# Seven-product scores for one more pair of query tiles in a causal attention and expert kernel

## The chip, the core and the metric

One core of a Trainium2 chip runs the whole program. Its engines are TensorE (PE, with weight loads as PEld), VectorE (DVE), ScalarE (ACT), GpSimd (POOL) and SyncE (SP), which here only issues DMAs. The metric is the time of one execution on the device in microseconds; less is better.

## The reference

All in float32. `x` has 2 batches of 2048 rows of 512. The normalised rows go through causal attention (with a norm of its own ahead of it) and through a mixture of 8 experts (width 352, the 2 best of each row); the result is `x + s * silu(experts)`.

```python
xn = _layernorm(x, axis=-1)
# attention
x_norm = (xn - mu) / jnp.sqrt(var + EPS) * gamma + beta
q, k, v = (x_norm @ qkv[:, i * KEY : (i + 1) * KEY] for i in range(3))
scores = jnp.einsum('bsk,btk->bst', q, k) * scale
scores = jnp.where(causal[None], scores, -jnp.inf)
attn = jax.nn.softmax(scores, axis=-1)
s = (attn @ v) @ o_proj + xn
# experts
h = jax.nn.silu(jnp.einsum('td,ehd->teh', xf, w1) + b1)
y = jnp.einsum('teh,edh->ted', h, w2) + b2
g = _silu(jnp.einsum('ted,te->td', y, comb))
x = x + s * g
```

## The kernel before

The program goes through norms and projections, then routing and experts (rows gathered by expert, 68 slots), and then the attention, the last 420 us or so. The change is in the attention alone.

**Tiles and steps.** A query tile is 128 rows. `seq` orders the 32 tiles, and the attention loop has a step `s` for each: the first batch's tiles 15 down to 0 in steps 0 to 15, then the second batch's in pairs, before in the order (8, 9), (0, 1), (6, 7), (2, 3), (4, 5), (10, 11), (12, 13), (14, 15), steps 16 to 31. Tile t needs keys 0 to t: whole blocks of 512 columns, and one cut block. `K` is 4, the first key block of the second batch, so K to K+3 are its four blocks.

**One step.** In step s TensorE makes the scores of tile s (`chunk_scores`, L994: four matmuls for a block), VectorE masks the last 128 columns (L999) and takes the maximum (L982), ScalarE takes the exponentials (`exponentials`, L1138). Their transpose is made in 16-bit halves: GpSimd splits them (`pu`, L1148), SP issues a transposing DMA (`puT`), and VectorE joins them in the next step (`join_p`, L1170). Tiles of at most 384 columns (`by_te`) are turned by TensorE instead (`turn_p`, L1165), with a copy back by ScalarE (L1166). The product with the values follows two steps after the scores (`values`, L1188).

**The end of a tile.** `gate` (L1343, L1344 on VectorE, then silu on ScalarE, L1346) combines the two gathered expert rows of a pair three steps after the pair's first tile, at the end of the step. `attended` (L1351 on ScalarE, then L1354 on VectorE) scales the attention's result three steps after its tile, and a step later `emit` (L1362, L1363 on GpSimd) multiplies and adds, and SP stores. `gather_y` (L1333) gathers expert rows from GpSimd's queue. exp and silu need different tables on ScalarE, so there is a table load at each change between them.

**Seven products.** For the pairs in `FAST` (0 to 3 and 13 to 15) scores against blocks 0 and 1 of a batch are made for two tiles at once as a 2 x 2 block product with seven products instead of eight (`fast_scores`, L1046, with additions on VectorE, L1052, and a copy of the first product by ScalarE, L1065). It needs four sums of the two tiles' queries (`query_sums`, L1013 to L1016) and four of the two key blocks (`block_sums`, L1027). The values of these pairs are multiplied in the same way (`values_first`, `values_next`, `values_end`, L1236), and need four sums for each value block (`combine_v`, L1210) and of the exponentials (`combine_p`, L1230).

**Buffers.** Products and scores lie in PSUM: pool `ps_a` has five banks of 128x512 float32, `ps_b` three. Each request takes the next bank of its pool and waits until the former content has been read. Before, products of steps after the third all use `ps_a`, so the sixth waits for the bank of the first. Keys have four buffers: block K's load takes the place of block 1 of the first batch, which tile 4 uses last, in step 11.

**Order.** It is written out by hand: each engine executes its instructions in the order in which the Python code gives them, and waits at the head of its queue. A step's code runs in this order: start of the step with loads of queries; `attended` and `emit` of earlier tiles; loads of `xo`; scores, with joins of the tile before between the blocks; `values` and `turn_p` where the tile before is short; the maximum's end (L1082); divisors; exponentials, with their DMAs; parts of key and value loads (`fetch_parts`, L794, at most four); the sums of keys and values that are due; the query sums for the next step; values; `gate`; `gather_y`. Before, value sums of K are made in step 20, of K+1 in step 22, of K+2 in step 26, and the key sums in steps 21 to 24, one in each:

```python
combine = {20: K, 22: K + 1, 26: K + 2}
...
            if s in combine:
                combine_v(combine[s])
            if 21 <= s < 25:

                block_sums(K, (s - 20,))
            if s % 2 and s > 3 and s // 2 + 1 in FAST:
                query_sums(s + 1, nc.vector)
```

In the second batch only pairs 13 to 15 use the sums.

Of the kernel before, what the change touches and what calls it, by code (L numbers as in the profile page):

```python
# [26 lines left out]
def gated_attention_moe(  # L27
# [27 lines left out]
    nc = tc.nc  # L55
# [752 lines left out]

    assert B == 2 and NBB == 4
    seq = [t for t in reversed(range(NBB * BT))]  # L810
    seq += [NBB * BT + t for t in (8, 9, 0, 1, 6, 7, 2, 3, 4, 5, 10, 11, 12, 13, 14, 15)]
    assert all(seq[s] // 2 == seq[s + 1] // 2 for s in range(0, NT, 2))
    fetch_k = fetch(aks, lambda: kp2, kt_d, "k2", "kT")
    fetch_v = fetch(avs, lambda: vp, v_d, "v2", "v")
# [142 lines left out]


    FAST = (0, 1, 2, 3, 13, 14, 15)

    def place(s):
        b, t = divmod(seq[s], BT)
# [21 lines left out]

    def direct(s):

        return range(2 if s // 2 in FAST else 0, len(widths[s]))

    def chunk_scores(s, j):
        b, t, first = place(s)  # L990
# [27 lines left out]
    def block_sums(first, parts=(1, 2, 3, 4)):  # L1018

        if 1 in parts:  # L1020
            bsums[first] = kt.tile([P, 4, ND // 2, TB], F32, name=f"tk_{first}", tag="tk")
        k = bsums[first]
        (b11, b12), (b21, b22) = ([aks[first + j][:, d, :] for j in range(2)] for d in kds)
        for i, x1, x2 in (1, b12, b11), (2, b22, k[:, 0]), (3, b22, b12), (4, b21, k[:, 1]):
            if i in parts:
                engine = nc.gpsimd if i == 3 and first == 0 else nc.vector
                engine.tensor_tensor(k[:, i - 1], x1, x2, ALU.subtract)  # L1027
# [103 lines left out]
    def exponentials(s):  # L1131

        _, nm, pieces = scored.pop(s)
        rs = sm.tile([P, NBB], F32, name=f"rs_{s}", tag="rs")
        sums[s], halves[s] = rs[:, : len(pieces)], []
        for j, (src, at) in enumerate(pieces):
            end = at + src.shape[1]
            nc.scalar.activation(  # L1138
                turned[s][:, at:end], src, AF.Exp, bias=nm, accum_out=rs[:, j : j + 1]
            )  # L1140
            if by_te(s):
                continue
            for k in range(at, end, TB):
                w = min(end - k, TB)

                pool, tag, n = (op, "xo", 4) if s == 1 else (php, "pu", 3)
                pu = pool.tile([P, 2 * TB], U16, name=f"pu_{s}_{k}", tag=tag, bufs=n)
                nc.gpsimd.tensor_copy(  # L1148
                    pu[:, : 2 * w].rearrange("p (h d) -> p h d", h=2),
                    turned[s][:, k : k + w].bitcast(U16).rearrange("p (d h) -> p h d", h=2),  # L1150
                )
                pool, tag, n = (op, "o", 4) if s == 1 else (php, "puT", 5)
                puT = pool.tile([P, 2 * BT, P], U16, name=f"puT_{s}_{k}", tag=tag, bufs=n)
                nc.sync.dma_start_transpose(out=puT[:, : 2 * w // P, :], in_=pu[:, : 2 * w])
                halves[s].append((puT, k, w))
# [170 lines left out]
    def gather_y(s):  # L1326

        rows[s] = [op.tile([P, 2, D], F32, name=f"yg0_{s}", tag="yg0")]
        for i in range(2):
            rows[s].append(op.tile([P, D], F32, name=f"yg1_{s + i}", tag="yg1"))  # L1330
            n = seq[s + i]
            for k, y in enumerate((rows[s][0][:, i, :], rows[s][-1])):
                nc.gpsimd.indirect_dma_start(  # L1333
                    out=y, out_offset=None, in_=y_d,
                    in_offset=bass.IndirectOffsetOnAxis(ap=posi[k][:, n : n + 1], axis=0),
                )
# [61 lines left out]
    parts_b = [(s, f, b, c) for s, f, b in parts_b for c in range(ND)]  # L1398
    parts_b.sort(key=lambda part: part[0])

    combine = {20: K, 22: K + 1, 26: K + 2}

    def fetch_parts(s, most):
        while parts_b and most and parts_b[0][0] <= s:
# [3 lines left out]

    for s in range(NT + OUT + 2):
        fast = s // 2 - 1 in FAST  # L1410
        pair = (s, s + 1) if s // 2 in FAST else (s,)
        if s < NT and (s % 2 == 0 or len(pair) == 1):
            for k in pair:
                if s:
                    begin_scores(k)
                room(k)
        n = s // 2 + 1
        if s % 2 == 0 and NQ <= n < NT // 2:
            for c in range(2):
                fetch_q(n, c)  # L1420
        if s == 0:
            fetch_parts(s, NBB * ND)
            block_sums(0)
        late = []
        for k in range(NT):
            if k not in AHEAD:
                wait = 4 - k % 2 if k // 2 in FAST else 3
                if s == k + wait:
                    late.append((attended, k))
                if s == k + wait + 1:  # L1430
                    emit(k)
        if len(pair) == 1 or s % 2:
            for f, *args in late:
                f(*args)
        for k in range(NT):
            if s == (NT - 1 if k in AHEAD else k + 2 - k % 2 if k // 2 in FAST else k + 1):
                fetch_inputs(k)
        if s == NT - 1:
            gather_y(NT - 2)
        joins = []  # L1440
        for k in () if s == 1 else (0, 1) if s == 2 else (s - 1,):
            if 0 <= k < NT - 1 and not by_te(k):
                joins += [(join_p, k)] * len(halves[k])
        chunks = []
        if s < NT and s != 1:
            chunks = [(k, j) for k in ((1,) if s == 0 else (s,)) for j in direct(k)]
        if s == 0:

            for k, j in chunks:
                chunk_scores(k, j)  # L1450
            chunks = []
        if s < NT and s % 2 == 0 and len(pair) == 2:
            pools = [(ps_b, "b")] * (NBB - 1) + [(ps_a, "a")] if s < 3 else [(ps_a, "a")]
            if s == 2:
                joins = [(combine_v, b, (1,)) for b in range(NBB - 1)] + joins
            now = 5 if s == 2 else 1
            fast_scores(s, pools, late + joins[:now])
            joins = joins[now:]
            if s == 0:
                query_sums(2, nc.gpsimd)  # L1460
        for k, j in chunks:
            chunk_scores(k, j)
            if s != 3 and joins:
                f, *args = joins.pop(0)
                f(*args)
        if s != 3:
            for f, *args in joins:
                f(*args)
        if 0 <= s - 1 < NT and by_te(s - 1):

            values(s - 2)
            turn_p(s - 1)
        if s < NT and s != 1:
            end_scores(s)
        if fast and s % 2 == 0 and 2 < s < NT:
            combine_p(s - 2)
        if 0 <= s - 1 < NT:
            divisor(s - 1)
        if s < NT:
            if s != 1:  # L1480
                exponentials(s)
            if s % 2 == 0 and len(pair) == 2:
                maximum(s + 1, turned[s + 1][:, : 2 * TB], 0)
            if s == 0:
                end_scores(1)
                exponentials(1)
            fetch_parts(s, 4)
            if s in combine:
                combine_v(combine[s])
            if 21 <= s < 25:  # L1490

                block_sums(K, (s - 20,))
            if s % 2 and s > 3 and s // 2 + 1 in FAST:
                query_sums(s + 1, nc.vector)
        if s == 2:
            pass
        elif s == 3:
            combine_p(0, (1, 3, 2))
            for b in range(NBB - 1):
                combine_v(b, (2,))  # L1500
            values_first(0)
            combine_p(0, (4,))
            for b in range(NBB - 1):
                combine_v(b, (4,))
            values_next(0)
            for f, *args in joins:
                f(*args)
            values_end(0, [lambda: query_sums(s + 1, nc.vector)])
        elif fast and s % 2 == 0:
            values_first(s - 2)  # L1510

            if s != NT - 2:
                values_next(s - 2)
        elif fast and s == NT - 1:
            values_next(s - 3)
            gate(s - 1)
            values_end(
                s - 3, [lambda: join_p(s)] * len(halves[s]) + [lambda: combine_p(s - 1)]
            )
            for k in AHEAD:  # L1520
                make_ahead(k)
        elif fast:
            values_end(s - 3)
        elif 0 <= s - 2 < NT and not (s - 1 < NT and by_te(s - 1)):
            values(s - 2)

        for k in range(0, NT - 2, 2):
            if s == (k + 2 if k + 2 in AHEAD else k + 3):
                gate(k)
        for k in range(0, NT - 2, 2):  # L1530
            if s == k + 1:
                gather_y(k)
        if s == 1:
            for b in range(NBB - 1):
                combine_v(b, (3,), nc.gpsimd)
# [45 lines left out]
```

## Time and profile before

| what | value |
|---|---|
| median of 3 runs | 1059.44 us (1057.37 to 1060.53) |
| the profiled execution | 1057.82 us |
| its span, first to last instruction | 1056.1 us |
| granted TensorE clock | 1.00 |
| TensorE idle, 860 to 890, 890 to 920, 920 to 950 us | 1.23, 1.30, 1.71 us |
| VectorE busy, 772 to 830 us | 33.1 of 58 us |
| VectorE busy, 830 to 950 us | 88.4 of 120 us |

Steps 12 to 15 run from about 795 to 820 us on TensorE, step 16 from 820, step 26 from 910, step 28 from 941.

Times of instructions are counted from the span's start. Where a line of the timeline names something in brackets, the engine stood idle for so long just before, and the name is what ended that. A float32 matmul is counted as two entries.

### The profile page before, as it was taken

What the parts mean: (1) busy time and instruction counts of PE and PEld (TensorE: products, weight loads), DVE (VectorE), ACT (ScalarE), POOL (GpSimd) and SP (SyncE); (2) the same over time, 40 slices, a digit from 0 to 9 for tenths busy, and PEclk for the clock granted to TensorE, in tenths of its full rate; (3) what the DMA queues carried; (4) which work ended last, traced back from release to release, by engine and by line L of the source; (5) the groups of instructions that cost most, each with busy time, mean ns of one, the idle gap of its engine ahead of it and who ended that gap; (6) DMA issues with size and microseconds to landing.
All of it is one profiled execution on the core that took longest, in us unless ns stands there. A gap on an engine that the chain in (4) does not pass through costs nothing.

```text
span 1056.1 us, 12196 instructions
## 1 busy us (share of the span) xinstructions
PE 1038.8 (98%) x3554; PEld 616.2 (58%) x3554; DVE 644.1 (61%) x1227; ACT 312.6 (30%) x643; POOL 432.4 (41%) x469
## 2 busy tenths in 40 slices
PE   8999999999999999999999999999999999899998
PEld 3687886444555555555545446676665544447577
DVE  4797884775333333334335459767655668688686
ACT  3222221211322322322355322122334443422330
POOL 2364250003433333334332127354547776754372
PEclk9999999999999999999999999999999999999999
DMA  8699989946999999999897257445668768744361
GB/s 302 180 283 282 282 263 339 340 142 171 221 221 227 222 233 228 223 232 218 207 187 159 58 191 180 118 101 139 184 169 270 214 202 231 185 112 120 96 156 40
DMA packets 300512, 209.33 MB, mean 198 GB/s; under 512 B 234520, under 2 KB 247576, under 8 KB 299424
## 3 DMA queue, kind: packets, MB, share of 16 engines
q1 hardware_dynamic: 281248, 146.12, 55.5%
q0 software_dynamic: 10560, 35.17, 13.0%
q10 hardware_dynamic: 8640, 27.27, 7.1%
q8 instruction: 30, 0.49, 0.2%
q14 instruction: 34, 0.28, 0.1%
HBM read 92.89 MB, written 60.03 MB: 145 GB/s over the span
## 4 chain that ended last, share of the span: by engine, by line
PE 77%; POOL 6%; issue 6%; DVE 5%; DMA 3%; ACT 2%; SPq 0%; ACTq 0%; POOLq 0%; DVEq 0%
PE py L921 16%; PE ph L882 15%; PE p L1236 9%; PE ps L994 8%; PE p L400 7%; PE p L1046 6%; PE pj L341 3%; PE pw L207 3%; PE po L1188 3%; PE pj L346 3%; PE p L1188 2%; POOL yg L1333 2%; POOL pu L1148 1%; DMA zuT<-zu 1%; POOL o L1362 1%
## 5 line engine op out<-in xcount | busy, mean ns | idle before, releaser
L921 PE MATMUL py<-w,ht 128*128 (+3 forms) x408 | 187.1, 594 | 0.0
L882 PE MATMUL ph<-w,xT 128*128 (+1 forms) x544 | 173.2, 460 | 0.7 <-POOL keep L1103 0.7
L929 DVE COPY y<-py 128x512 f32<-128x512 f32 x68 | 46.9, 690 | 179.0 <-PE py L921 172.9
L994 PE MATMUL ps<-k,q 128*128 128x512 f32 (+3 forms) x416 | 143.0, 495 | 0.0
L882 PEld LDWEIGHTS ph<-w,xT 128*128 128x128 f32 (+1 forms) x544 | 97.5, 181 | 73.1 <-issue 34.5
L907 ACT ACTIVATE ht<-ht,b1sel 128x128 f32<-128x128 f32 (+3 forms) x237 | 73.1, 375 | 224.1 <-DVE ht L901 224.1
L892 POOL COPY hu<-h 128x704 uint16<-128x704 uint16 x68 | 52.4, 771 | 204.1 <-ACT h L890 124.7
L1148 POOL COPY pu<-pT 128x1024 uint16<-128x1024 uint16 (+2 forms) x74 | 84.0, 1167 | 126.3 <-ACT pT L1138 67.3
L921 PEld LDWEIGHTS py<-w,ht 128*128 128x128 f32 (+3 forms) x408 | 73.4, 182 | 75.4 <-issue 37.4
L994 PEld LDWEIGHTS ps<-k,q 128*128 128x128 f32 x416 | 74.6, 190 | 67.6 <-issue 57.7
L768 POOL DMA_INDIRECT xs<-zu_d,toki x68 | 68.9, 1014 | 69.3 <-DVE toki L642 57.9
L1188 PE MATMUL po<-v,pT 128*128 128x512 f32 x182 | 81.2, 593 | 1.2 <-DVE pT L1170 1.2
L1333 POOL DMA_INDIRECT yg<-y_d,posi x64 | 64.2, 1003 | 36.5 <-DVE yg L1344 22.1
L264 POOL COPY zu<-z 128x1024 uint16<-128x1024 uint16 x32 | 35.2, 1100 | 78.0 <-DVE z L249 78.0
L1170 DVE COPY pT<-puT 128x1024 uint16<-128x1024 uint16 (+2 forms) x74 | 55.9, 787 | 7.4 <-DMA puT<-pu 7.4
L1188 PEld LDWEIGHTS po<-v,pT 128*128 128x128 f32 x182 | 34.0, 190 | 40.0 <-issue 37.8
L413 DVE TENSOR_TENSOR so<-p,so 128x512 f32<-128x512 f32 x70 | 45.8, 686 | 16.5 <-DMA v_d<-so 9.3
L1354 DVE SCALAR_TENSOR_TENSOR o<-xo,xscale,o 128x512 f32<-128x512 f32 x30 | 28.7, 962 | 41.9 <-ACT o L1351 17.3
L842 DVE COPY xT<-xhT 128x1024 uint16<-128x1024 uint16 x68 | 47.2, 693 | 10.6 <-PE ph L882 5.7
L1052 DVE TENSOR_TENSOR pT<-p,pT 128x512 f32<-128x512 f32 x49 | 32.8, 687 | 25.5 <-PE p L1046 13.8
L1362 POOL TENSOR_TENSOR o<-o,yg 128x512 f32<-128x512 f32 x30 | 41.8, 1393 | 13.5 <-DVE o L1354 12.5
L1138 ACT ACTIVATE pT<-ps,nm 128x512 f32<-128x512 f32 (+3 forms) x52 | 30.0, 581 | 56.6 <-DVE nm L1082 37.3
(246 smaller groups left out, 1670.5 us busy)
## 6 DMA issues: line engine op xcount, KB each, us to landing
y_d<-y SPq DMA_DIRECT2D x68, 256.0 KB
zu_d<-zu SPq DMA_DIRECT2D x32, 264.0 KB
x<-in_x_dram SPq DMA_DIRECT2D x32, 256.0 KB
kt_d<-kT ACTq DMA_DIRECT2D x8, 1024.0 KB
k<-kt_d SPq DMA_DIRECT2D x32, 256.0 KB
q<-qt_d SPq DMA_DIRECT2D x32, 256.0 KB
v<-v_d SPq DMA_DIRECT2D x32, 256.0 KB
xo<-in_x_dram SPq DMA_DIRECT2D x32, 256.0 KB
```

Of the source, the lines that this page charges most:

```text
L400: nc.tensor.matmul(ps[:, r, :], lhsT=lhs[:, c, ts(r, P)], rhs=rhs[:, c, :], start=(c == 0), stop=(c == 1),)
L768: nc.gpsimd.indirect_dma_start(out=xs, out_offset=None, in_=zu_d, in_offset=bass.IndirectOffsetOnAxis(ap=toki[:, i : i + 1], axis=0),)
L882: nc.tensor.matmul(ph[at, :], lhsT=xT[:, c, at], rhs=rhs[k], start=(c == 0), stop=(c == ND - 1),)
L907: nc.scalar.activation(ht[:hn, c, at], ht[:hn, c, at], AF.Silu, bias=b1sel[:hn, c, j : j + 1])
L921: nc.tensor.matmul(py[at, :], lhsT=ht[:k, c, at], rhs=rhs[n], start=(c == 0), stop=(c == NH - 1),)
L994: nc.tensor.matmul(ps[:, :w], lhsT=aqs[seq[s] // 2][:, c, ts(t % 2, P)], rhs=aks[first + j][:, c, :w], start=(c == 0), stop=(c == ND - 1),)
L1046: nc.tensor.matmul(ps, lhsT=x[:, c], rhs=y[:, c], start=(c == 0), stop=(c == ND // 2 - 1))
L1148: nc.gpsimd.tensor_copy(pu[:, : 2 * w].rearrange("p (h d) -> p h d", h=2), turned[s][:, k : k + w].bitcast(U16).rearrange("p (d h) -> p h ...
L1170: nc.vector.tensor_copy(turned[s][:, k : k + w].bitcast(U16).rearrange("p (i t h) -> p i t h", t=P, h=2), puT[:, : 2 * w // P, :].rearrang ...
L1188: nc.tensor.matmul(dst, lhsT=turned[s][:, ts(k, P)], rhs=avs[first + k // BT][:, k % BT, cols], start=(start and k == k0), stop=(k == k1 - 1),
L1236: nc.tensor.matmul(dst, lhsT=a[:, k], rhs=v(k), start=(k == 0), stop=(stop and k == n - 1))
L1333: nc.gpsimd.indirect_dma_start(out=y, out_offset=None, in_=y_d, in_offset=bass.IndirectOffsetOnAxis(ap=posi[k][:, n : n + 1], axis=0),)
```

## The change

Five things change.

1. Pair 8 (tiles 8 and 9 of the second batch, steps 16 and 17) gets its scores against blocks 0 and 1 by seven products (`SCORED`), in step 16; its values stay as they were. Step 17's joins of tile 16 move behind its exponentials (`behind`).
2. The short tiles 0 and 1 change places with tiles 6 and 7: they come in steps 20, 21 instead of 18, 19.
3. The sums of keys and values of the second batch are spread (`later`): values of K+2 in steps 10, 11 and 12 (one, one, two), keys in 13, 14 and 15 (one, two, one), values of K+1 in 17 to 20 and of K in 20 to 23, one in each step.
4. The query sums for a pair go ahead of the joins and scores of the step before it, instead of to its end.
5. In the seven products of steps after the third, the sixth takes a bank of `ps_b`.

```diff
@@ -808,7 +808,7 @@
-    seq += [NBB * BT + t for t in (8, 9, 0, 1, 6, 7, 2, 3, 4, 5, 10, 11, 12, 13, 14, 15)]
+    seq += [NBB * BT + t for t in (8, 9, 6, 7, 0, 1, 2, 3, 4, 5, 10, 11, 12, 13, 14, 15)]
@@ -957,6 +957,7 @@
     FAST = (0, 1, 2, 3, 13, 14, 15)
+    SCORED = FAST + (8,)
@@ -984,7 +985,7 @@
-        return range(2 if s // 2 in FAST else 0, len(widths[s]))
+        return range(2 if s // 2 in SCORED else 0, len(widths[s]))
@@ -1398,7 +1399,13 @@
-    combine = {20: K, 22: K + 1, 26: K + 2}
+    later = {}
+    for steps, f, b in (
+        ((10, 11, 12, 12), combine_v, K + 2), ((13, 14, 14, 15), block_sums, K),
+        ((17, 18, 19, 20), combine_v, K + 1), ((20, 21, 22, 23), combine_v, K),
+    ):
+        for i, step in enumerate(steps):
+            later.setdefault(step, []).append((f, b, (i + 1,)))
@@ -1408,7 +1415,7 @@
-        pair = (s, s + 1) if s // 2 in FAST else (s,)
+        pair = (s, s + 1) if s // 2 in SCORED else (s,)
@@ -1437,10 +1444,16 @@
+        if s % 2 and s > 3 and s // 2 + 1 in SCORED:
+            query_sums(s + 1, nc.vector)
         joins = []
...
+        behind = []
+        if s % 2 and s // 2 in SCORED and s // 2 not in FAST:
+
+            behind, joins = joins, []
@@ -1450,7 +1463,9 @@
-            pools = [(ps_b, "b")] * (NBB - 1) + [(ps_a, "a")] if s < 3 else [(ps_a, "a")]
+            pools = [(ps_a, "a")] * 5 + [(ps_b, "b"), (ps_a, "a")]
+            if s < 3:
+                pools = [(ps_b, "b")] * 3 + [(ps_a, "a")]
@@ -1479,19 +1494,16 @@
             if s != 1:
                 exponentials(s)
+            for f, *args in behind:
+                f(*args)
...
             fetch_parts(s, 4)
-            if s in combine:
-                combine_v(combine[s])
-            if 21 <= s < 25:
-
-                block_sums(K, (s - 20,))
-            if s % 2 and s > 3 and s // 2 + 1 in FAST:
-                query_sums(s + 1, nc.vector)
+            for f, *args in later.pop(s, []):
+                f(*args)
```

## The prediction

> **What bounds the kernel now.** I read the busy shares first, then TensorE's waits, then its timeline from 810 us on, and then the other engines' timelines at the same times.
>
> ```profile
> PE 1038.8 (98%) x3554; PEld 616.2 (58%) x3554; DVE 644.1 (61%) x1227; ACT 312.6 (30%) x643; POOL 432.4 (41%) x469
> ...
> PE p L1046 <- ACT yg L1346: 1.7, 1, 1.7
> ...
> PE p L1046 <- DVE sq L1014: 1.3, 1, 1.3
> PE po L1188 <- DVE pT L1170: 1.2, 1, 1.2
> ...
> PE p L1046 <- ACT pT L1065: 0.4, 1, 0.4
> ```
>
> The span is TensorE's. A change pays only by removing matmuls or one of these few stalls, and costs as soon as it makes a new one. Columns of a wait: total, times, longest.
>
> The price of seven products comes from the chain of waits (one fp32 matmul counts as two entries):
>
> ```profile
> 674.45 12.02 PE p L1046 x28
> ```
>
> So 14 matmuls of 128x512 take 12.02 us, 0.859 us each.
>
> What decides is how tight steps 13 to 16 are. Timeline (start, duration, what; in brackets the idle before), SyncE, VectorE, ScalarE, GpSimd, TensorE:
>
> ```profile
> 806.42 1.23 SPq L1154 DMA_TRANSPOSE puT<-pu  x1
> 807.71 2.01 SPq L794 DMA_DIRECT2D k<-kt_d  x4
> ...
> 810.52 0.47 DVE L1343 TENSOR_SCALAR yg<-yg,share 128x512 f32<-128x512 f32 x1
> ...
> 812.21 0.75 DVE L1344 SCALAR_TENSOR_TENSOR yg<-yg,share,yg 128x512 f32<-128x512 f32 x1
> 816.11 1.26 DVE L1354 SCALAR_TENSOR_TENSOR o<-xo,xscale,o 128x512 f32<-128x512 f32 x1 [3.15 <-ACT yg L1346]
> ...
> 813.06 1.28 ACT L1346 ACT_TABLE_LOAD   x1 [1.95 <-DVE yg L1344]
> 814.35 1.06 ACT L1346 ACTIVATE yg<-yg 128x1024 f32<-128x1024 f32 x1
> 815.32 0.76 ACT L1351 ACTIVATE o<-po,xshift,ri 128x512 f32<-128x512 f32 x1
> 816.67 0.48 ACT L1166 COPY pT<-pt 128x384 f32<-128x384 f32 x1 [0.60 <-PE pt L1165]
> ...
> 815.52 1.28 POOL L1362 TENSOR_TENSOR o<-o,yg 128x512 f32<-128x512 f32 x1
> ...
> 817.31 2.74 PE L1188 MATMUL po<-v,pT 128*128 128x512 f32 x6
> 820.11 7.92 PE L994 MATMUL ps<-k,q 128*128 128x512 f32 x24
> ```
>
> Read down: gate(10) on VectorE ends at 812.96, silu(10) with its table load follows, then attended(11), then the copy of tile 13's transpose, which ends at 817.15. TensorE uses it at 817.31. There are 0.6 us between attended(11) and that copy; any greater delay of gate(10) is a stall of TensorE.
>
> **What the Trainium skill says.** "SBUF — State Buffer", Who interferes with whom: a VectorE instruction with two SBUF inputs and a GpSimd instruction that reads SBUF exclude each other for the whole instruction. The trace agrees: the attended operation at 816.11 takes 1.26 us beside the GpSimd operation that ends at 816.80, and 0.75 us elsewhere; the query sum at 914.96 takes 1.26 instead of 0.42. "ScalarE: Activation LUTs", What ACT_TABLE_LOAD costs: 1.28 us, as here, at each change between silu and exp. "DMA: Bandwidth & Descriptors", Anatomy of one DMA: about 2 us are fixed; here a 256 KB xo load issued at 803.36 releases VectorE at 806.00. "PSUM — Partial Sum Buffer", The four PSUM rules: a product of 512 fp32 columns fills a bank, so five banks of ps_a hold five products, which the 1.7 us wait above shows: product six waits for the copy of product one.
>
> **The gains.** (Line numbers are those of before.)
> - Pair 8 (steps 16, 17) needs 14 matmuls instead of 16 for blocks 0 and 1: 2 x 0.859 = -1.7 us.
> - The stall of 1.2 us at 887.5 is values(20) waiting for a join that stands behind a late attended operation (2.19 us at 883.52). With the short tiles in steps 20, 21, tile 20 is turned by TensorE and has no join: -1.2. Tiles 6, 7 take steps 18, 19, and their four transposes on SP now stand ahead of keys 7's four loads. They have about 24 us from score to use: nothing.
> - In step 26, 1.3 (query sums behind a join that waits 2.13 us for its DMA) and 1.7 us (copy of product one behind silu(22)). Three key sums of 1.2 us and eight value sums of 0.7 us leave steps 20 to 23, one value sum a step returns, and the query sums (4 x 0.42) go ahead of the joins; VectorE is 3 to 5 us earlier: -3.0. The same for 0.4 us in step 28. The query sums of step 5 move into 4.3 us of idle VectorE: nothing.
> - The sixth product's other bank: no gain by itself, since the seventh needs product one's bank 1.7 us later. In steps 28 to 31 it turns the ring of three banks by one; what is then waited for was read some 10 us before: nothing.
> - The value sums of keys K+2 leave step 26 for steps 10 to 12. See the next part for those of steps 11 and 12.
>
> Sum: -6.3 us.
>
> **The costs.** They follow one chain, which I worked through by order of instructions and rows of the profile.
> 1. *Step 11.* A value sum of 0.68 us stands ahead of gate(8), where VectorE and GpSimd alternate (a GpSimd operation ends at 793.04, two copies follow). It waits for the first, gate(8) ends at about 797.8 instead of 796.0. Silu(8), attended(9) and step 12's joins follow; exp(12), its GpSimd copy, its transpose on SP and the four key loads behind that on SP come 0.7 to 2.2 us later. I take 2.2.
> 2. *Step 13.* The first key sum (L1027, 1.21 us) stands ahead of gate(10) and reads the first two quarters of keys 4. In before these are issued from 807.71; 512 KB have moved by 811.4 and, with the 0.65 us that a transpose needed from its last byte to its join, they are usable at 812.0; with 2.2 us, at 814.2. Sum until 815.4, gate(10) (2.45) until 817.8 instead of 812.96, 4.8 later. Less the slack of 0.8 (0.6 ahead of the copy, 0.2 behind it), TensorE stands 4.0 us at L1188 in step 15. Floor: no delay in step 11, 812.0 + 1.21 + 2.45 = 815.7, which is 2.7 later, a stall of 1.9.
> 3. *Steps 14, 15.* Ahead of the query sums that product three needs stand attended(11), the mask and maximum, key sums two and three (2 x 1.21), attended(12), two query sums (0.84). From attended(11) on ScalarE (A) that is A + 5.9; TensorE wants it at A + 6.9 (copy 0.5, two handoffs, values 2.6, turn 0.3, products one and two 3.4). Without disturbance: no stall. But silu(10) releases four GpSimd operations of 1.27 us, of which VectorE meets three to four: 3 us later, a stall of 2.1 us at L1046. Product four also needs the bank that exp(15) frees, about as late.
> 4. *Step 16.* Key sum four (1.21) and gate(12) (2.45) stand ahead of silu(12), and that ahead of the copy of product one: it ends 17.4 us after A, and product seven is due at 15.9 (the 2.1 included): 1.6 us more with the handoff. Floor of 3 and 4 together 0.5, ceiling 4.5.
> 5. *Step 18.* Tile 16's exponentials now wait for the products' sums: copy + 3.4 (five adds) + 0.75 + 0.7 + 1.2 (maximum of 1024) + 0.7 + 0.75 = 7.5, exp 1.15, then 4.5 to the first join, as in before (832.17 to 836.72), + 0.7. TensorE wants it 13.0 us after the copy (product seven 1.7, then 11.3 of other matmuls): 13.8 - 13.0 = 0.8 us, between 0 and 1.6. The new step 17 puts these joins behind the exponentials, so they delay no maximum.
>
> VectorE's nine more instructions (1.2 us and less) are in this chain. Sum: 4.0 + 2.1 + 1.6 + 0.8 = +8.5, between 2.4 and 11.
>
> **The sum.** -6.3 + 8.5 = +2.2 us on the profiled execution: 1057.8 (span 1056.1 and 1.7 around it) becomes 1060.0. That execution lies 1.6 us below the median 1059.4; against the median, 1061.6.
>
> **The rivals.**
> - *The gain arrives.* If step 11's sum delays nothing and GpSimd's four operations meet VectorE's gaps (it stands idle 3.15 us at 812.96 and 1.25 at 818.5), costs are 2.4 to 3.1: -6.3 + 2.7 = -3.6, 1055.8. For it: every added operation fits in VectorE's idle time by size. Against: that idle time is waiting on ScalarE, and the additions stand ahead of what ScalarE waits for.
> - *The shared SBUF read port decides* (slower). Place: VectorE between attended(11) and the query sums of step 15. If GpSimd wins each turn, key sums two and three, attended(12) and the first query sum each wait 1.27 us, and tile 16's joins meet the copies for tile 17 likewise: costs 3 to 5 rise by 3, +5.2, 1064.6. It decides from the first GpSimd operation beyond the 1.0 us of slack. For it: 883.52, where an attended operation took 2.19 us. Against: usually VectorE gets every second turn.
> - *The change doesn't do what it says at step 26*: its stalls return because VectorE is late throughout: 3.0 more than the forecast, 1064.6. Against: 9 us of sums left these steps, 3 came back. It is inside the slower case.
>
> **How the numbers follow.** 0.3% (3.2 us) is about what a measurement can tell from no change. Forecast (between -3.2 and +3.2): 0.48. Gain arrives: 0.20. Slower by the port, a longer load of keys or joins: 0.32. The range 1056 to 1065 spans -3.4 to +5.6; the forecast's own is 1056.2 to 1062.6.
>
> **What would show it.** TensorE's waits after: the three of steps 22 and 26 gone; new ones at L1188 (on ScalarE's copy) near 817 us of 2 to 4 us, at L1046 on the query sums or exp(15), and on the copy of product one. VectorE's first key sum starts on a DMA of keys 4 after 812. Wrong if tile 13's copy still ends near 817.2, if product three doesn't wait, or if the stalls of step 26 remain.

## The result and the profile after

The changed kernel takes 1064.22 us (median of 6, 1063.2 to 1066.11) against 1059.59 us of the kernel before (6 runs): a ratio of 1.0052, 95% interval 1.0039 to 1.0064. It is slower by 4.6 us. Its profiled execution took 1064.46 us, span 1062.8.

The page's first part and TensorE's waits, after (a line of code has moved by one in this region, so L1188 of before is L1189):

```profile
PE 1039.7 (98%) x3550; PEld 615.9 (58%) x3550; DVE 663.2 (62%) x1236; ACT 312.1 (29%) x640; POOL 433.9 (41%) x469
...
PE po L1189 <- ACT pT L1167: 2.9, 1, 2.9
PE p L1237 <- DVE u L1254: 2.1, 1, 2.1
...
PE po L1189 <- ACT pT L1139: 1.3, 1, 1.3
PE po L1189 <- DVE pT L1171: 1.2, 1, 1.2
PE p L1047 <- ACT pT L1066: 1.1, 2, 0.8
PE p L1047 <- ACT pT L1139: 1.0, 1, 1.0
```

TensorE has two matmuls fewer (four entries), and yet is busy 0.9 us longer: 0.55 of it lie ahead of step 10, and behind that the 1.7 us saved and the 1.8 us of a slow clock, shown below, nearly cancel. VectorE is busy 19 us longer. Of the waits of before, the one on silu (1.7) and the one on the query sums (1.3) are gone from the list. Of the six lines shown three are new (2.9, 1.3, 1.0), two have grown (0.6 to 2.1, 0.4 to 1.1), and the 1.2 on a join is as long as before, in another step.

The stages ahead of the attention, which the change does not touch, differ from one execution to the next: the scores of step 10 start at 773.12 us before and at 775.07 after. From the first of the seven products of step 0 to there it is 156.5 us in both executions. So executions are compared here from that point to the end of the span as well, called the *rest* below: 282.98 us before, 287.73 after, +4.75, close to the +4.63 of the medians. TensorE's timeline accounts for it:

| place | before | after | difference |
|---|---|---|---|
| pair 8, 14 matmuls for 16 | | | -1.7 |
| step 22 of before, join (887 us) | 1.2 | 0 | -1.2 |
| step 28, copy of product one | 0.4 | 0 | -0.4 |
| steps 25 and 26, waits around the seven products | 3.0 | 2.5 | -0.5 |
| step 15, wait for the copy of tile 13's transpose | 0 | 2.9 | +2.9 |
| step 15, the six entries after it | 2.74 | 4.54 | +1.8 |
| step 16, copy of product one | 0 | 0.8 | +0.8 |
| step 18, joins of tile 16 | 0 | 1.3 | +1.3 |
| step 31, sums of the values' products | 0.6 | 2.1 | +1.5 |
| sum | | | +4.5 |

The new stall of step 15, in the timeline of after. To set these times beside those of before, take off 1.95 us:

```profile
810.52 2.01 SPq L794 DMA_DIRECT2D k<-kt_d  x4
...
815.18 1.23 DVE L1028 TENSOR_TENSOR tk<-k,k 128x1024 f32<-128x1024 f32 x1 [1.77 <-DMA k<-kt_d]
...
818.03 0.75 DVE L1345 SCALAR_TENSOR_TENSOR yg<-yg,share,yg 128x512 f32<-128x512 f32 x1
...
818.88 1.28 ACT L1347 ACT_TABLE_LOAD   x1 [4.96 <-DVE yg L1344]
820.17 1.06 ACT L1347 ACTIVATE yg<-yg 128x1024 f32<-128x1024 f32 x1
821.14 0.76 ACT L1352 ACTIVATE o<-po,xshift,ri 128x512 f32<-128x512 f32 x1
...
821.80 0.47 ACT L1167 COPY pT<-pt 128x384 f32<-128x384 f32 x1
...
822.32 4.54 PE L1189 MATMUL po<-v,pT 128*128 128x512 f32 x6 [2.90 <-ACT pT L1167]
```

The first key sum waits 1.77 us for the keys. The gate stands behind it and ends at 818.78. Then come silu, attended and the copy, one after the other, and by then TensorE has stood idle for 2.90 us. Its next six entries take 4.54 us instead of 2.74. The view by windows says why (the third number from the end is the granted clock):

```profile
824.00:825.00 1.00, 1.00 (x3) 0.35 (x2) 0.97 (x4) 0.94 (x3) 1.00 (x2) 0.50 0.00 0
...
826.00:827.00 1.00, 1.00 (x6) 0.47 (x5) 1.00 (x1) 0.00 (x0) 0.92 (x2) 1.00 0.90 268
```

TensorE worked at half its clock just after the idle time, and had the whole of it again from 826 us on.

### The profile page after: what moved, and what is told of

The parts are those of the page before. It is cut to its first block, busy times and chain, and to the rows that moved or that the text cites. A ratio compares the mean times of both kernels' runs of the same rounds, so it can differ in the third digit from the quotient of the medians.

```text
span 1062.8 us, 12200 instructions
## 1 busy us (share of the span) xinstructions
PE 1039.7 (98%) x3550; PEld 615.9 (58%) x3550; DVE 663.2 (62%) x1236; ACT 312.1 (29%) x640; POOL 433.9 (41%) x469
## 4 chain that ended last, share of the span: by engine, by line
PE 65%; DMA 8%; POOL 8%; DVE 7%; issue 7%; SPq 2%; ACT 2%; ACTq 0%; POOLq 0%; DVEq 0%
PE py L921 16%; PE ph L882 15%; PE p L1237 9%; PE p L1047 7%; PE ps L995 7%; PE pw L207 3%; DMA w<-in_w_t_dram 2%; PE p L1189 2%; PE pj L341 2%; DMA zuT<-zu 2%; PE po L1189 2%; SPq L271 2%; POOL yg L1334 1%; PE pj L346 1%; POOL o L1363 1%
## 5 line engine op out<-in xcount | busy, mean ns | idle before, releaser
L995 PE MATMUL ps<-k,q 128*128 128x512 f32 (+3 forms) x384 | 129.3, 487 | 0.0
L995 PEld LDWEIGHTS ps<-k,q 128*128 128x128 f32 x384 | 68.6, 190 | 60.4 <-issue 50.5
L1189 PE MATMUL po<-v,pT 128*128 128x512 f32 x182 | 83.1, 604 | 5.4 <-ACT pT L1167 2.9
L1189 PEld LDWEIGHTS po<-v,pT 128*128 128x128 f32 x182 | 34.5, 193 | 45.6 <-issue 39.2
L1053 DVE TENSOR_TENSOR pT<-p,pT 128x512 f32<-128x512 f32 x56 | 37.4, 687 | 28.6 <-PE p L1047 16.7
L1355 DVE SCALAR_TENSOR_TENSOR o<-xo,xscale,o 128x512 f32<-128x512 f32 x30 | 32.2, 1079 | 34.0 <-ACT o L1352 18.2
L1139 ACT ACTIVATE pT<-pT,nm 128x1024 f32<-128x1024 f32 x16 | 18.4, 1149 | 108.7 <-DVE nm L1083 70.3
```

The lines of the kernel that those rows point to most:

```text
L995: nc.tensor.matmul(ps[:, :w], lhsT=aqs[seq[s] // 2][:, c, ts(t % 2, P)], rhs=aks[first + j][:, c, :w], start=(c == 0), stop=(c == ND - 1),)
L1189: nc.tensor.matmul(dst, lhsT=turned[s][:, ts(k, P)], rhs=avs[first + k // BT][:, k % BT, cols], start=(start and k == k0), stop=(k == k1 - 1),
```

## The experiments

Three questions were open. What makes step 15 late: the places of the key sums (theory A), or pair 8's seven products (theory B)? Why do waits at steps 25 and 26 stay: is VectorE late there because of the order of the tiles (theory C), or because of the sums put into steps 20 to 23? And where does the wait of step 31 come from? Ratios are to the kernel before on the same chip; *rest* is that of the one profiled execution (282.98 for before, 287.73 for after). Where the two differ, as in e8, the ratio decides, since it rests on all executions.

| run | what it is | median us | ratio (95% interval) | rest us |
|---|---|---|---|---|
| e1_direct16 | after, pair 8 with eight products | 1061.06 | 1.0025 (1.0010 to 1.0040) | 283.8 |
| e2_gate_first | after, key sums behind the gates | 1060.49 | 1.0012 (0.9998 to 1.0027) | 284.3 |
| e3_old_order | after, tiles in the old order | 1067.04 | 1.0078 (1.0058 to 1.0098) | 291.3 |
| e4_query_bank | before, with parts 4 and 5 of the change | 1058.98 | 0.9998 (0.9986 to 1.0009) | 282.5 |
| e5_filled | after, three products more in the idle time of step 15 | 1064.98 | 1.0042 (1.0027 to 1.0057) | 287.2 |
| e6_values26 | e2, values of K in step 26 | 1062.15 | 1.0014 (1.0001 to 1.0026) | 284.5 |
| e7_old_spread | e6 with eight products and the old order | 1063.59 | 1.0042 (1.0026 to 1.0058) | 287.8 |
| e8_new_spread | e6 with eight products | 1059.32 | 1.0003 (0.9989 to 1.0016) | 280.6 |
| e9_behind | after with eight products, all sums behind gates | 1057.66 | 0.9985 (0.9973 to 0.9998) | 279.9 |
| e10_turn | after, two small reductions ahead of gate(28) | 1062.50 | 1.0038 (1.0026 to 1.0050) | 285.9 |
| e11_bank4 | e9, the other bank for product four | 1057.32 | 0.9984 (0.9973 to 0.9996) | 279.9 |
| e12_behind_turn | e9 with e10's reductions | 1055.33 | 0.9958 (0.9941 to 0.9974) | 278.6 |

### Pair 8 and the key sums

e1_direct16 takes the seven products of pair 8 away:

```diff
-    SCORED = FAST + (8,)
+    SCORED = FAST
```

> The changed kernel with pair 8's scores made directly again (16 matmuls); sums, order of tiles, query sums and bank as changed. Theory A (the key sum that waits for keys 4 ahead of gate(10) in step 13 costs most: a stall of 2.9 us in step 15 and a slowed TensorE clock after it, 1.8 us): stall and slow clock stay; only the waits on product one's copy (0.8) and on tile 16's exponentials (1.3) go and 1.7 us of matmuls come back, so about 1063.8 us, 0.4 below the changed kernel. Theory B (the seven products themselves, with their longer way to tile 16's exponentials, cost most): 1059 us or less.

e2_gate_first keeps them, and makes the key sums of a step after its gate:

```diff
-            for f, *args in later.pop(s, []):
-                f(*args)
+            for f, *args in later.get(s, []):
+                if f is not block_sums:
+                    f(*args)
...
                 gate(k)
+        for f, *args in later.pop(s, []):
+            if f is block_sums:
+                f(*args)
```

> The changed kernel with the key sums of steps 13 and 15 put behind gate instead of ahead of it (step 14 has no gate). Theory A: the stall of step 15 and the slow clock go (4.7 us), the copy of product one comes 1.2 us earlier, the query sums may make product three wait by up to 1.6: 1058.5 to 1060.5 us. Theory B: the products' waits stay, 1062 us or more.

In e1 the wait of step 15 is as long as in the changed kernel, 2.88 us: the seven products do not make it. But those of steps 16 and 18 and the one at 914 us are gone, and the ratio falls from 1.0052 to 1.0025 (the two intervals just meet). So each theory has its part. In e2 the wait of step 15 has gone, and the ratio falls from 1.0052 to 1.0012, with intervals apart: the place of the key sums costs some 4 us. TensorE's timeline shows what was next:

```profile
829.20 5.42 PE L1047 MATMUL p<-tk,sq 128*128 128x512 f32 x12 [1.58 <-DVE sq L1015]
...
850.75 7.96 PE L1189 MATMUL po<-v,pT 128*128 128x512 f32 x18 [1.31 <-ACT pT L1139]
```

The first is the wait of product three for pair 8's query sums, the second that of step 18 for tile 16's joins. Both belong to pair 8, and together they are larger than the 1.7 us that its two saved matmuls are worth. e6 and e8 below, which differ by `SCORED` alone, point the same way: 1.0014 with the seven products, 1.0003 without (these intervals overlap). Their rests, 284.5 and 280.6, differ by more, but 1.6 us of that is the wait of step 31, which has another cause (see the last experiments). At this place the seven products cost more than they save.

### The slow clock that hid a wait

In e2 product three waits for the query sums; in the kernel after it doesn't. The suspicion is that the slow clock after the idle time gave the sums the time they needed. e5_filled puts three products that nobody uses into the idle time:

```diff
         po = ps_b.tile([P, D], F32, name=f"po_{s}", tag="b")
+        if s == 13:
+            product(po, 12, 0, 3, slice(0, D))
         product(po, s, 0, place_keys(s), slice(0, D))
```

> The changed kernel with three additional products of tile 12 (2.6 us of TensorE work whose result is overwritten) put ahead of tile 13's products with the values in step 15, that is, into the idle 2.9 us. Theory (the slow clock hid another wait): the stall there shrinks to about 0.3 us, the six entries of tile 13 take 2.7 us again instead of 4.5, and 1.5 to 1.8 us of waiting for the query sums appear at product three in their place; the time stays that of the changed kernel, 1063.5 to 1065. Rival (the slow clock is a loss by itself): no new wait behind it, about 1062.2.

```profile
824.99 2.84 PE L1191 MATMUL po<-v,pT 128*128 128x512 f32 x6 [0.46 <-ACT pT L1167]
...
832.81 5.42 PE L1047 MATMUL p<-tk,sq 128*128 128x512 f32 x12 [1.32 <-DVE sq L1015]
```

With TensorE kept busy the six entries take 2.84 us, and 1.32 us of waiting for the query sums stand where the slow clock had been. The rest is 287.2 us, 0.5 below that of after, and that 0.5 is a shorter wait in step 31 (1.58 for 2.11). So the 1.8 us of slow clock were no loss of their own in this kernel: take it away and the next late thing costs as much. e3 below shows it without a filling: after 3.10 us of idle time at the same place the clock stayed whole, the six entries took 2.84 us, and product three then waited 1.33 us for the query sums.

### The order of the tiles and the waits of step 26

e3_old_order puts the short tiles back:

```diff
-    seq += [NBB * BT + t for t in (8, 9, 6, 7, 0, 1, 2, 3, 4, 5, 10, 11, 12, 13, 14, 15)]
+    seq += [NBB * BT + t for t in (8, 9, 0, 1, 6, 7, 2, 3, 4, 5, 10, 11, 12, 13, 14, 15)]
```

> The changed kernel with the tiles in the old order (short tiles 0, 1 in steps 18, 19). Theory C (with the short tiles in steps 20 and 21, TensorE needs only 8.6 us for steps 22 and 23 while VectorE and ScalarE need 14 us for a pair, so the waits of 2.5 us in steps 25 and 26 stay although the sums left): these waits go (-2.5), but 5.1 us of matmuls no longer cover tile 16's joins, whose wait grows from 1.3 to 6.4, and the wait of 1.2 at step 22 comes back: about 1068 us. Rival (VectorE is late in steps 25 and 26 for another reason, and tile 16's joins have room): 1063 to 1065 us, with the waits of steps 25 and 26 unchanged.

```profile
852.29 10.90 PE L1189 MATMUL po<-v,pT 128*128 128x512 f32 x18 [6.43 <-ACT pT L1139]
...
1033.59 2.86 PE L1237 MATMUL p<-vT,pT 128*128 128x256 f32 x12 [0.65 <-DVE u L1254]
```

From 850 us on these two lines are the only ones of e3's TensorE timeline with idle time in brackets: the waits of steps 22 to 28 are all gone, also the one of step 22 that was expected back, and the one of step 31 is at 0.65. But with short tiles right behind tiles 8 and 9, TensorE has nothing to do while tile 16's joins are made (6.43 us, and 10.90 instead of 7.96 us after them). These 9 us also give VectorE time to catch up, so e3 alone does not show that the order makes the waits of steps 25 and 26. e7_old_spread has the old order, eight products, the key sums behind the gates, and all four value sums of K in step 26.

> The old order of tiles and the old scores of pair 8, but the sums spread: key sums behind the gates of steps 13 to 15, value sums of keys K in step 26, query sums early, the sixth bank. If the sums' places alone were worth what the prediction gave them: the 3.0 us at step 26 go and nothing comes, 1059.3 - 3.0 = about 1056. Rival (VectorE's chain by pairs sets the pace): 1058 to 1059.5.

Neither case came: only 0.2 us is left at step 26, but two waits for joins (1.5 and 3.9 us) stand in steps 18 and 19, with a slow clock after the second; 1.0042. So the old order and early sums do not go together. e8 below differs from e7 by the order alone and has 1.0003, with intervals apart: the new order pays there. But it leaves TensorE less to do ahead of step 26: from the scores of step 20 to the first product of step 26 it needed 52 us before (858.4 to 910.3) and 42 us after (876.1 to 917.8), since tiles 6 and 7 are now done earlier. VectorE and ScalarE have three pairs to bring through on the way in both. From the end of one gate to that of the next, after shows 15.5, 14.0 and 18.6 us. VectorE in the shortest of these:

```profile
893.56 0.75 DVE L1345 SCALAR_TENSOR_TENSOR yg<-yg,share,yg 128x512 f32<-128x512 f32 x1
897.44 1.27 DVE L1355 SCALAR_TENSOR_TENSOR o<-xo,xscale,o 128x512 f32<-128x512 f32 x1 [3.13 <-DMA q<-qt_d]
...
899.87 1.74 DVE L1211 TENSOR_TENSOR vT<-v 128x512 f32<-128x512 f32 x1
...
904.58 0.67 DVE L1211 TENSOR_TENSOR vT<-v,vT 128x512 f32<-128x512 f32 x1
...
907.52 0.75 DVE L1345 SCALAR_TENSOR_TENSOR yg<-yg,share,yg 128x512 f32<-128x512 f32 x1
```

From the end of one gate (894.31) to that of the next (908.27) are 13.96 us: 3.13 us of waiting while silu and then attended run on ScalarE (the bracket names a DMA, but ScalarE's part of attended ends at 897.40, just ahead of the row), two attended operations, the maxima, and two value sums, which stand ahead of the next gate and cost 2.4 us here. e6_values26 takes e2 and moves the four value sums of K:

```diff
-        ((17, 18, 19, 20), combine_v, K + 1), ((20, 21, 22, 23), combine_v, K),
+        ((17, 18, 19, 20), combine_v, K + 1), ((26, 26, 26, 26), combine_v, K),
```

> The changed kernel with its key sums behind the gates and the four value sums of keys K back in step 26 instead of steps 20 to 23. Theory (VectorE is short of time in steps 20 to 25, and the value sums put there, 4.8 us with their waits for the port, are what makes it late): the waits of 1.2, 1.0 and 0.3 us around step 26 go, 1060.5 - 2.5 = about 1058. Rival (the chain gate, silu, attended, maximum sets the pace whatever else VectorE does): they stay, about 1060.5.

```profile
PE p L1047 <- ACT pT L1139: 1.0, 1, 1.0
PE p L1237 <- DVE s L1231: 1.0, 1, 1.0
...
PE p L1047 <- ACT pT L1066: 0.8, 2, 0.5
```

Of the 2.5 us the wait for the join (1.2) went. Product four's wait for its bank (1.0) stayed, and 1.5 us came in step 28 (0.5 of the last line, and the second), where the moved sums now make VectorE late. The ratio is that of e2. e8_new_spread is e6 with eight products for pair 8 ("the same" in its text is e7):

> The same with the new order of tiles. If the order pays (the 1.2 us wait of step 22 goes) but step 31 loses 1.5 us: about the same as with the old order, 1056 to 1057. If pair 8's seven products pay by themselves, this is 1 to 2 us slower than the version with seven products and the same sums; if the waits that they bring (1.6 at the query sums, 1.3 at tile 16's joins) eat their 1.7 us, it is 1 us faster.

It is level with the kernel before: 1.0003.

### The query sums and the sixth bank alone

e4_query_bank is the kernel before with the query sums ahead of the joins, and the other bank for product six.

```diff
+        if s % 2 and s > 3 and s // 2 + 1 in FAST:
+            query_sums(s + 1, nc.vector)
         joins = []
...
-            pools = [(ps_b, "b")] * (NBB - 1) + [(ps_a, "a")] if s < 3 else [(ps_a, "a")]
+            pools = [(ps_a, "a")] * 5 + [(ps_b, "b"), (ps_a, "a")]
+            if s < 3:
+                pools = [(ps_b, "b")] * 3 + [(ps_a, "a")]
...
-            if s % 2 and s > 3 and s // 2 + 1 in FAST:
-                query_sums(s + 1, nc.vector)
```

> The kernel before with two parts of the change alone: query sums ahead of the step's joins, and the other bank for the sixth product. If the forecast of the gains was right in kind: the waits of 1.3, 1.7 and 0.4 us at L1046 go, 1056.2 us. Rival (VectorE's lateness at steps 24 and 25 comes from gate and silu, which stay where they are): the 1.3 goes and the others come back at the next product or its bank: 1058 to 1059 us.

The 3.0 us of step 26 became 0.7 and 0.3 us, but 1.0 us came in step 28 at the value products and 0.1 at step 31; the rest is 0.5 us shorter, and the ratio 0.9998. The bank does matter, then: the copy of product one ends hardly earlier than it did (11.7 us after product one starts, 11.9 before), but product seven waits for it, one product later than product six did. And the early query sums have a price: they stand ahead of the maxima of step 25, so the exponential of its first block ends 5.9 us after product one starts instead of 4.4, and product four waits for the bank that it reads, in this run and in every run with the new order but e11.

### Sums where VectorE waits anyway

VectorE stands idle for some 3.1 us after a gate while ScalarE makes silu. e9_behind makes all sums right behind a gate, in odd steps alone, and pair 8 with eight products:

```diff
-        ((10, 11, 12, 12), combine_v, K + 2), ((13, 14, 14, 15), block_sums, K),
-        ((17, 18, 19, 20), combine_v, K + 1), ((20, 21, 22, 23), combine_v, K),
+        ((11, 11, 11, 11), combine_v, K + 2), ((13, 13, 15, 15), block_sums, K),
+        ((17, 17, 19, 19), combine_v, K + 1), ((21, 21, 23, 23), combine_v, K),
...
-            for f, *args in later.pop(s, []):
-                f(*args)
...
                 gate(k)
+        for f, *args in later.pop(s, []):
+            f(*args)
```

> The changed kernel without the seven products of pair 8, with every sum behind the gate of its step: value sums of keys K+2 in step 11, key sums two each in steps 13 and 15, value sums of keys K+1 in steps 17 and 19 and of keys K in steps 21 and 23. Theory (a sum costs nothing where VectorE waits for silu, 3.1 us after each gate, and costs where it stands ahead of a gate or of other work): no wait in steps 15 to 22, those of steps 27 and 28 (0.5 and 1.0 us in the run with the sums in step 26) gone, in all about 4 us below the kernel before in the attention, so about 1056. Rival (a sum is a load on VectorE wherever it stands, and the pairs' chain passes it on): 1058.5 to 1059.5, with waits of 2 us or more left at steps 22 to 26.

No wait is left in steps 15 to 25 nor in 27 to 30, and 0.9 us in step 26; the ratio of 0.9985 (0.9973 to 0.9998) is below 1 with its whole interval. That is a gain of about 1.6 us; the rest of the profiled execution is 3.1 us shorter, and about 4 had been expected. The wait of step 31 stayed, at 2.1 us. e11_bank4 gives the other bank to product four:

```diff
-            pools = [(ps_a, "a")] * 5 + [(ps_b, "b"), (ps_a, "a")]
+            pools = [(ps_a, "a")] * 3 + [(ps_b, "b")] + [(ps_a, "a")] * 3
```

> The same with the other bank for product four instead of product six. Theory (product four waits for the bank that the exponential of tile 25 holds): the wait of 0.6 to 1.0 us there goes, and what is left is 0.3 us at product seven: 0.7 us less than with the bank at product six. Rival (the copy of product one is then due earlier): the wait moves to product six or seven, no difference.

The rival holds: product four's wait goes, and the last product waits 1.1 us instead of 0.3 for the copy of product one. The rest is 279.9 us in both.

### Who gets the turn in step 30

In the first three profiles with the new order (after, e1, e2) TensorE waits 2.1 us in step 31, in those with the old order (before, e3, e4) 0.6 or 0.7. But the order is not the cause, as e8 shows: it has the new order and does not wait there at all. Before, then after:

```profile
1008.20 1.55 DVE L1343 TENSOR_SCALAR yg<-yg,share 128x512 f32<-128x512 f32 x1
1008.20 1.26 POOL L1362 TENSOR_TENSOR o<-o,yg 128x512 f32<-128x512 f32 x1
...
1018.85 0.49 DVE L1343 TENSOR_SCALAR yg<-yg,share 128x512 f32<-128x512 f32 x1
```

```profile
1013.37 0.48 DVE L1344 TENSOR_SCALAR yg<-yg,share 128x512 f32<-128x512 f32 x1
1013.41 1.56 POOL L1363 TENSOR_TENSOR o<-o,yg 128x512 f32<-128x512 f32 x1
...
1024.46 3.96 DVE L1344 TENSOR_SCALAR yg<-yg,share 128x512 f32<-128x512 f32 x1 [1.14 <-DMA yg<-y_d,posi]
...
1025.13 3.00 POOL L1149 COPY pu<-pT 128x1024 uint16<-128x1024 uint16 x3
...
1030.78 2.86 PE L1237 MATMUL p<-vT,pT 128*128 128x256 f32 x12 [2.11 <-DVE u L1254]
```

Before, gate(28) and a multiplication of GpSimd are ready together, and GpSimd goes first (0.49 us of work take VectorE 1.55). After, VectorE is ahead by 0.04 us and goes first. All fourteen profiles sort by this turn. Where VectorE starts at most 0.02 us ahead (before, e3, e4, e7, e8), or behind (e10, e12), this operation takes it 1.45 to 1.57 us, and the wait of step 31 is 0 to 0.7 us. Where it is 0.04 to 0.07 us ahead (after, e1, e2, e5, e6, e9, e11), it takes 0.48 us, and the wait is 1.6 to 2.1 us. When VectorE has gone first, as in after, GpSimd ends its operations later (1019.72, 2.9 us after TensorE's group of 1016.85, against 2.3 us before), so the gathers behind them are issued later, gate(30) waits for their DMA, and starts next to three copies: 3.96 us. "SBUF — State Buffer" of the Trainium skill, Who interferes with whom, says that the engine that issues first holds the pair of ports that the two share for its whole instruction, and that the other is blocked. The rows agree with it, and the 3.96 us, which end 0.29 us after the third copy, show a block over several instructions. e10_turn gives VectorE two small reductions to do first:

```diff
+        if s == 30:
+            late_by = cp.tile([P, 2], F32, name="late_by", tag="late_by", bufs=1)
+            for i in range(2):
+                nc.vector.tensor_reduce(late_by[:, i : i + 1], sums[s - 2], AX.X, ALU.max)
         for k in range(0, NT - 2, 2):
```

> The changed kernel with two more reductions of one column (0.14 us each) ahead of gate(28) in step 30, nothing else. Theory (the 1.5 us of step 31 are a matter of turns: gate(28) starts 0.04 us ahead of a GpSimd operation and takes its turn, so everything up to step 31's gate comes in another sequence, and that gate's scaling is then shut out by three copies): gate(28) loses the turn as in the kernel before, the 3.96 us scaling is 0.5 to 1.5 us again, the wait of 2.1 us falls to 0.6 to 0.7, and 1062.7. Rival (step 31 is late for another reason): the wait stays at 2.1 and the time at 1064.2 or above.

```profile
1009.82 1.27 POOL L1363 TENSOR_TENSOR o<-o,yg 128x512 f32<-128x512 f32 x1
1009.88 1.48 DVE L1344 TENSOR_SCALAR yg<-yg,share 128x512 f32<-128x512 f32 x1
...
1020.74 0.60 DVE L1344 TENSOR_SCALAR yg<-yg,share 128x512 f32<-128x512 f32 x1 [0.20 <-issue]
...
1025.13 2.86 PE L1237 MATMUL p<-vT,pT 128*128 128x256 f32 x12
```

GpSimd has the turn again, the scaling takes 0.60 us, and TensorE does not wait. The ratio goes from 1.0052 to 1.0038 (the intervals overlap), the rest from 287.7 to 285.9 us. More work on VectorE, and 1.9 us less in the profiled execution. e12_behind_turn puts the same into e9:

> The version with all sums behind the gates and without the seven products of pair 8, with the two small reductions ahead of gate(28). Theory (the turn of step 30 decides step 31 whatever came before): the wait of 2.1 us at step 31 goes, 1057.7 - 2.1 = about 1055.6, faster than the kernel before by 3 us or more. Rival (the turn depends on the sums as well): the wait stays between 0.6 and 2.1, 1056.2 to 1057.7.

```profile
PE p L1237 <- DVE u L1254: 0.7, 1, 0.7
PE p L1047 <- ACT pT L1139: 0.6, 1, 0.6
...
PE p L1047 <- ACT pT L1066: 0.3, 1, 0.3
```

That is all that is left of TensorE's waiting from step 10 on. 1055.33 us, 0.9958 (0.9941 to 0.9974): 4 us faster than the kernel before, and about 9 below the median of the changed one. It has parts 2, 4 and 5 of the change, part 3 at other places, and not part 1.

## Why the prediction was wrong

It put the sum at +2.2 us and called no clear change the likeliest; +4.6 us was measured. By its steps:

- **The step that failed is the gain in step 26**, "-3.0": the waits of steps 25 and 26 came to 2.5 us instead of 3.0, a gain of 0.5. The reason given was that VectorE would be 3 to 5 us earlier there. It was not. Before, then after, the first product, the exponential whose bank product four takes, and the copy of product one:

```profile
910.30 3.60 PE L1046 MATMUL p<-k,q 128*128 128x512 f32 x8
914.02 0.69 ACT L1138 ACTIVATE pT<-ps,nm 128x512 f32<-128x512 f32 x1 [5.48 <-DVE nm L1082]
921.67 0.57 ACT L1065 COPY pT<-p 128x512 f32<-128x512 f32 x1
```

```profile
917.80 3.60 PE L1047 MATMUL p<-k,q 128*128 128x512 f32 x8
923.32 0.69 ACT L1139 ACTIVATE pT<-ps,nm 128x512 f32<-128x512 f32 x1 [6.62 <-DVE nm L1083]
929.24 0.57 ACT L1066 COPY pT<-p 128x512 f32<-128x512 f32 x1
```

Counted from the start of the first product, the copy ends at 11.9 us before and at 12.0 after. Only in e3 and e7, behind their long waits, is it clearly earlier, by 1.7 and 1.3 us; in the other runs it ends at 11.5 to 12.0 us. So the 1.7 us at product six did not go because VectorE was earlier: with the other bank it is product seven that needs the copy, 1.7 us later, and 0.3 of waiting stays. The 1.3 us for the query sums went too, but these sums, 3.7 us long here and not 1.7, now stand ahead of the maxima of step 25: the exponential ends at 6.2 us instead of 4.4, and product four waits 1.0 for its bank. And a wait of 1.2 for a join is new in step 25. It went when the sums moved (e6), when the seven products went (e1) and with the old order (e3), so it has no single cause. Two things that the prediction did not count bear on it, with shares that were not separated: TensorE needs 10 us less from step 20 to step 26, and the sums that came back were longer. The two of step 20 and the three of steps 21 to 23 took 6.3 us (1.43, 1.75, 0.67, 1.74, 0.67), not 3, as three of them met GpSimd. The rival that named this place, "The change doesn't do what it says at step 26", was put at 3.0 us and inside the slower case; it was worth 2.5.
- **Step 31 had no term**, and cost 1.5. It hangs on one turn between two engines, decided within some 0.04 us, as e10, e12 and the sorting of all profiles show. With the 2.5 of step 26 it is more than the whole difference between forecast and result.
- **Step 11** (2.2 later) was too large: the key loads were issued 0.9 us later than before, measured from the scores of step 10.
- **Step 13** was right in its mechanism, each link as described: the key sum started on the DMA of keys 4, at 813.23 on the clock of before (foreseen between 812.0 and 814.2), and the stall at L1188 was 2.9 us, between the floor of 1.9 and the 4.0 taken. e2 shows that the place of the key sums makes it.
- **Steps 14 and 15** (2.1 at the query sums) came as 1.8 us of slow clock ahead of them instead, and as 1.3 us of waiting where the clock stays up (e5, e3).
- **Step 16** gave 0.8 for 1.6, **step 18** 1.3 for 0.8. In all the costs are 6.8 for 8.5.
- **The smaller gains** are as said: 1.7 for the matmuls, 1.2 in step 22, 0.4 in step 28. The 1.2 us did not stay away: the same kind of wait, for a join, is among the 2.5 us.
- **The sixth bank** "no gain by itself" does not fit its own reason: if product seven comes 1.7 us later, a wait for the same copy shrinks by up to 1.7 us, and the traces show this at step 26. In e4 the bank and the early query sums take 2.0 us out of step 26, and half of that comes back in step 28. The two were not tried apart.

So gains of 3.8 instead of 6.3, costs of 6.8 instead of 8.5, and 1.5 not foreseen: +4.5. Of the three signs of being wrong two came: product three does not wait in the changed kernel, and stalls of step 26 remain. That the time lies inside the range of 1056 to 1065 is in part luck, since the costs were put 1.7 us too high. So is its closeness to the 1064.6 us of the two slower rivals: the one on the port wanted 3 us more of cost where there was 1.7 less, and the one on step 26, right in its place, had those costs too high and no term for step 31.

## What to carry to other kernels

Where work of one engine is moved out of a stretch, count what the bounding engine loses there too: here VectorE lost sums and TensorE lost 10 us of matmuls, and VectorE was no earlier against it. Moving sums ahead makes whatever stands behind them later, as the query sums did to the maxima. Sums for an in-order engine cost no wait here where that engine waits for another one (behind a gate, during silu), and the same sums ahead of the gate cost a stall. A saving of matmuls that puts additions, copies and joins on the way to the next ones must be charged with these: pair 8's seven products saved 1.7 us, and their two waits in e2 were 2.9.

## What was not expected of the hardware

The clock of TensorE fell to half in short idle times, and not in every one. With 2.90 us of idle time (after) the clock was half for about 3.4 us, and six entries took 4.54 us; after 2.88 us (e1) and 3.10 us (e3, step 15) they took 2.84; after 3.20 us (e10) 5.49. The longest wait, in e3, by windows:

```profile
845.86:852.29 6.43, 0.00 (x1) 0.03 (x1) 4.66 (x9) 3.02 (x9) 5.97 (x6) 0.66 0.47 92
852.30:857.00 4.70, 4.70 (x6) 2.10 (x7) 4.67 (x6) 0.00 (x0) 4.12 (x4) 0.50 0.95 199
```

In the first line the mean clock is 0.66 over 6.43 us of idle time, so it was half for about 4.4 of them: it fell about 2.1 us after TensorE had stopped. In e10 too it fell after 2.1 us, in after and e7 after 3.0 and 3.6 us. In windows of 0.1 us the half clock then lasts 3.4 us in after and e7, 6.8 in e10 and 10.2 in e3. "TensorE: Matmul & The Clock Gate" of the Trainium skill, Part 1: The HAM clock gate, describes half the clock after an idle window of about 3.4 us, full clock after a busy one, and windows that run freely. The 0.50 agrees, and the lengths are once, twice and three times the page's 3.4 us. That a window must be idle for its whole length does not agree with a fall after 2.1 us, and here the measurement decides; what share of a window is enough was not measured, nor where the windows lay.

That one idle time slows the clock and another of the same length does not makes such a stall hard to price. It is not shown to be what makes times uneven: the 16 runs of e1, which has the stall, lie between 1055.94 us at a mean clock of 1.000 and 1066.77 at 0.994, but the 18 runs of e2, which lacks it, lie between 1055.54 at 1.000 and 1064.64 at 0.997, and 58 runs of the kernel before between 1055.74 at 1.000 and 1064.4 at 0.996.
